# A graph layer on one core: SyncE fetches one of eight tiles of source rows of every eleventh chunk, row by row at addresses from registers

## The chip, the core and the metric

One core of a Trainium2 chip runs the whole kernel. The time is that of the device in microseconds, the median of the runs shown; a profile of one execution goes with it. TensorE is PE here (PEld its weight loads), VectorE DVE, ScalarE ACT, GpSimd POOL, and SyncE, which only issues DMAs, SP.

## What is computed

A graph with 6,250 nodes of 128 features and 200,000 edges, sorted by their destination. The layer is pre-normalized: `h = relu(layernorm(x))`, then two mesh convolutions and one edge-weighted attention, and the result is added to `x`. Cut to what matters:

```python
def mesh_conv(x, src, dst, ea, w1, b1, g, bt, w2, b2):
    m = concat([x[dst], x[src], ea]) @ w1 + b1        # per edge
    m = silu(group_norm(m, g, bt)) @ w2 + b2
    return segment_sum(m, dst) / clip(count(dst), 1)
...
q, k, v = h @ qw + qb, h @ kw + kb, h @ vw + vb
logits = (q[dst] * k[src]).sum(-1) * scale + ea @ ew + eb
w = softmax of logits over the edges of each dst
o = segment_sum(w * v[src], dst) @ ow + ob
```

The products with `w1` are done per node, so an edge needs the row of its source out of a table in DRAM: 128 numbers (512 bytes) in the convolutions, keys and values (1 KB) in the attention. The source is random, the destination sorted.

## The kernel before

**Tiles.** The edges stand in tiles of 128 (an edge a partition), 1,563 in all, and eight tiles make a chunk: 196 chunks, the last of three tiles. Three stages go over all chunks: `conv(1)`, `conv(2)` (L1003) and the attention (L1206 on). Each runs `pipeline` (L744), whose loop takes one step a chunk: it fetches the chunk two ahead, does the first product of the next chunk, the first half of this one, and the second half of older ones, and now and then a piece of a node batch (finished nodes, four windows of 128, every eighth step in the later part of a stage). At its end `in_order` (L732) fixes the order of DVE, SP, ACT and PE as written.

**Source rows.** `gather` (L648) issues one indirect DMA on POOL per tile (L650), which reads 128 indices from `src_i` in SBUF and fetches a row for each into tile `g`. POOL isn't in the list of `in_order`; it runs ahead as far as buffers allow: four of `g` in the convolutions, eleven in the attention. In the convolutions DVE adds `g` to the product (L1046); in the attention DVE multiplies its first half with the queries (L1258) and its second with the weights (L1314).

**Destination rows.** `loads` (L626) is SP's part of a step. It loads a register with the chunk's first node (`value`, L607) and fetches 112 rows from there into one of three tiles `pk` (L636). Every second step `load_group` (L614) loads for two chunks the relative destinations, broadcast to 112 partitions (`ohT`, L620, 896 KB), and the edge attributes (L623). ACT turns them into a one-hot matrix (`compared`, L645 and L646), and PE multiplies the two (L1039, in the attention L1243). PE also sums the edges of each node (L1071 and L1321). In the attention SP also loads, every eight steps, 16 rows of masks back to back (`load_runs`, L1272). SP also reads and stores the tables of the node batches (L882 to L948).

**Order on SP.** SP issues in program order. Where a DMA must wait for a buffer (L636 for a product of the chunk that used `pk` before, L620 for the group before last), all later ones wait behind it. The DMAs that SP issues take their completion semaphores in turn from eight, so that each also waits for the one eight before it.

Of the kernel before, what the change touches and what calls it, by code (L numbers as in the profile page):

```python
# [8 lines left out]
FP = mybir.dt.float32  # L9
BF = mybir.dt.bfloat16  # L10
I32 = mybir.dt.int32
# [4 lines left out]
SP = mybir.EngineType.SP  # L16
# [5 lines left out]
P = 128  # L22
D = 128
# [4 lines left out]
TPC = 8  # L28
# [4 lines left out]
LG = 2  # L33
WN = 112
SOON = 24
TAILS = [7, 7, 6, 5, 4, 3, 4]
BY_ACT = 60
KE = 5
KW = WN + KE
DB = D + H  # L40
PITCH = D + 4
VK = H * (HD + 1)
KV = 2 * D
# [6 lines left out]
def kernel(ctx: ExitStack, tc: tile.TileContext, x, src, dst, eat, w, out):  # L50
# [9 lines left out]
    nc = tc.nc  # L60
    N = x.shape[0]
    EI = src.shape[1]
    NCH = -(-EI // TPC)
# [5 lines left out]
    const = ctx.enter_context(tc.tile_pool(name="const", bufs=1))  # L69
# [7 lines left out]
    hpc = gpc.enter_context(tc.tile_pool(name="hpc", bufs=1))  # L77
# [43 lines left out]
    rows = {}  # L121

    def load_row(queue, name):
        v = w[name]
        rows[name] = const.tile([P, D], FP, name=f"r_{name}")
        queue.dma_start(
            out=rows[name], in_=bass.AP(tensor=v.tensor, offset=v.offset, ap=[[0, P], [1, D]]))

# [15 lines left out]
    b_d = {i: dram.tile([NW * P, D], FP, name=f"b_d{i}") for i in (1, 2)}  # L144
    kv_d = dram.tile([NW * P, KV], FP, name="kv_d")
    wc_d = {i: dram.tile([KE, D], FP, name=f"wc_d{i}") for i in (1, 2)}
    web_d = dram.tile([KE, DB], FP, name="web_d")
    dwl_d = dram.tile([P, EW], FP, name="dwl_d")
# [46 lines left out]
    with tc.tile_pool(name="node0", bufs=1) as np_, tc.tile_pool(name="prep", bufs=1) as pp, \  # L195
# [8 lines left out]
        step = 8  # L204
# [38 lines left out]
        for a in range(0, NW, 4):  # L243
            m = min(4, NW - a)
# [17 lines left out]
            o = pso.tile([P, 4, P], FP, name="o")  # L262
# [24 lines left out]
        for a, (m, tT) in keep.items():  # L287
            o = pso.tile([P, 4, P], FP, name="o")
# [50 lines left out]
        nc.vector.memset(t, 0.0)  # L339

    temb = hpc.tile([P, D], FP, name="temb")
    squares = {n: const.tile([P, D], FP, name=f"w_{n}") for n in ("c1_w2", "c2_w2", "ow")}
    qkv_t = const.tile([P, 3, D], FP, name="qkv_t")

    def spread(i):

        sizes, n = (TAILS[::-1], G) if i == 3 else ([GC] + [1] * 4, GC)
        rest, out = NCH, []
        while rest:
            out.insert(0, min(rest, sizes.pop(0) if sizes else n))  # L350
            rest -= out[0]
        return out

    def steps_of(i):


        ends, due, n = {}, {}, 0
        for m in spread(i):
            ends[n + m] = list(range(n, n + m))
            due.setdefault(n + m + (n < NCH - (sum(TAILS) if i == 3 else SOON)), []).extend(ends[n + m])  # L360
            n += m
        waiting, todo, left = [], [], NCH
        while left:
            n = len(todo)
            waiting += due.get(n, ())
            steps = min([m for m in due if m > n], default=n + 1) - n
            k = -(-len(waiting) // steps)
            todo.append(waiting[:k])
            waiting = waiting[k:]
            left -= k  # L370
        return ends, todo
# [239 lines left out]
    class Chunk:  # L611
        oh = None

    def load_group(c, pools):  # L614

        n = min(LG, NCH - c)
        m = min(n * TPC, EI - c * TPC)
        t = pools["ohT"].tile([P, LG, EPC], FP, name="ohT")
        f = t.rearrange("p c e -> p (c e)")
        nc.sync.dma_start(  # L620
            out=f[:WN, :m * P],
            in_=rel_d[c * TPC:c * TPC + m, :].rearrange("t p -> (t p)")[None, :].to_broadcast([WN, m * P]))
        nc.sync.dma_start(out=f[WN:KW, :m * P], in_=eat[:, c * EPC:c * EPC + m * P])  # L623
        pools[c // LG] = t
# [20 lines left out]
        nc.scalar.activation(k.ohT[:WN, :], k.ohT[:WN, :], AF.Square, bias=minus_p[:WN])  # L645
        nc.scalar.activation(k.ohT[:WN, :], k.ohT[:WN, :], AF.Relu, bias=1.0, scale=-4.0)  # L646

    def gather(k, g, table_d):  # L648
        for t in range(k.nt):
            nc.gpsimd.indirect_dma_start(  # L650
                out=g[:, t, :table_d.shape[1]], out_offset=None, in_=table_d,
                in_offset=bass.IndirectOffsetOnAxis(ap=k.src[:, t:t + 1], axis=0))
# [20 lines left out]
    def leftovers(body, pools):  # L673
# [9 lines left out]
        def one(c):  # L683
# [3 lines left out]
            with tc.For_i(0, n, 1) as r:  # L687
                k = Chunk()
                k.nt = TPC
                k.ea = lp.tile([KE, EPC], FP, name="l_ea")  # L690
                if isinstance(c, int):
# [52 lines left out]
    def pipeline(i, stage, aside=iter(())):  # L744

        start = len(nc.cur_bb.bb.instructions)
        ends, todo = steps_of(i)
        starts = {n: j for j, (n, _) in enumerate(plans[i])}
        ahead = stage.ahead
        ks, under_way, said = {}, [], {}
        for c in range(ahead):
            ks[c] = stage.fetch(c)
            compared(ks[c])
        stage.products(ks[0])
        for n, seconds in enumerate(todo):  # L760
            if n + ahead < NCH:
                ks[n + ahead] = stage.fetch(n + ahead)
            if n + 1 < NCH and stage.soon:
                stage.products(ks[n + 1])
            run = [ks[c] for c in ends.get(n, ())]
            stage.root(run)
            if n + ahead < NCH and stage.soon:
                compared(ks[n + ahead])
            first = (lambda k: lambda: stage.first(k))(ks[n]) if n < NCH else None
            if stage.second(run, [ks.pop(c) for c in seconds], first) and first:  # L770
                first()
            stage.finish()
            if n + ahead < NCH and not stage.soon:
                compared(ks[n + ahead])
            if n + 1 < NCH and not stage.soon:
                stage.products(ks[n + 1])
            if n < NCH:
                stage.early(ks, n, todo[n + 1])
            if n in starts:
                for _ in aside:  # L780
                    pass
                under_way.append(stage.batch(starts[n]))
            for g in list(under_way):
                if said.get(g) == "held" and n + 1 in ends:
                    continue
                said[g] = next(g, STOP)
                if said[g] is STOP:
                    under_way.remove(g)
            if n > 4:
                next(aside, None)  # L790
            if n < NCH:
                stage.reduce(ks[n])
        stage.flush()
        for g in (*under_way, aside):
            for _ in g:
                pass
        in_order(start)


    class Nodes:  # L800


        def __init__(self, pool, bank):
            self.pool, self.bank = pool, bank
# [198 lines left out]
    def conv(i):  # L1003
# [4 lines left out]
        with ExitStack() as es:  # L1008
            pool = lambda n, b, **kw: es.enter_context(tc.tile_pool(name=f"{n}{i}", bufs=b, **kw))
            pools = {"ohT": pool("ohT", 2), "oh": pool("oh", 2),  # L1010
                     "ps": pool("ps", 1, space=PSUM)}
# [12 lines left out]
                nc.vector.tensor_copy(t, s)  # L1024
            np_, nd = pool("np", 1), pool("nd", 1, space=PSUM)
            nodes = Nodes(np_of(np_, "A", "o"), lambda: nd.tile([P, BN, D], FP, name="nd", tag="nd"))
            side = es.enter_context(ExitStack())
            aside = iter(())
            if i == 1:
# [53 lines left out]
            class Stage:  # L1083
                ahead, soon = 2, True
                sums, late, roots, next = [], [], False, 0
                var, j, sd = None, 0, None

                def fetch(self, c):
                    k = loads(c, pools, a_d[i], self.ahead)
                    k.g = gp.tile([P, TPC, D], FP, name="g")  # L1090
                    gather(k, k.g, b_d[i])
                    k.h = hs[c % len(hs)]
                    return k

# [68 lines left out]
                    add_late(self.sums[0])  # L1163

            stage = Stage()
            nodes.var = lambda: stage.var[:, NV:]
            pipeline(i, stage, aside)
            side.close()
            pools["left"] = pool("left", 1)

            wcl = pools["left"].tile([KE, D], FP, name="wcl")
            nc.sync.dma_start(out=wcl, in_=wc_d[i])
# [28 lines left out]

    conv(1)
    conv(2)
    gpc.close()

# [5 lines left out]
    with ExitStack() as es:  # L1211
        pool = lambda n, b, **kw: es.enter_context(tc.tile_pool(name=f"{n}a", bufs=b, **kw))
        pools = {"oh": pool("oh", 2), "ps": pool("ps", 1, space=PSUM)}
# [156 lines left out]
        class Stage:  # L1370
            ahead, soon = 2, False
            sums, late, nb = [], [], None
            lg, j = None, 0

            def __init__(self, bp):
                self.bp = bp
                self.runs = list(steps_of(3)[0].values())
                self.nb = load_runs(self.runs.pop(0), bp)

            def fetch(self, c):  # L1380
                k = loads(c, pools, a_d[3], self.ahead)
                k.g = gp.tile([P, TPC, KV], FP, name="g")
                gather(k, k.g, kv_d)
                return k

            def products(self, k):
# [13 lines left out]
            def early(self, ks, n, then):  # L1400

                if then and then[0] >= NCH - BY_ACT:
                    onehot_by_act(ks[then[0]])
# [62 lines left out]
                merge_late(self.sums[0])  # L1466
                add_late(self.sums[0])

        with tc.tile_pool(name="bpa", bufs=1) as bp, tc.tile_pool(name="ohTa", bufs=2) as pools["ohT"]:
            pipeline(3, Stage(bp))  # L1470

        pools["left"] = pool("left", 1)
        webl = pools["left"].tile([KE, DB], FP, name="webl")
        nc.sync.dma_start(out=webl, in_=web_d)
# [79 lines left out]
```

## Time and profile before

| | |
|---|---|
| runs | 8,065.72, 8,086.02 and 8,091.16 us; median 8,086.02 |
| the profiled execution | 8,089.77 us, of which its span is 8,088.0 |
| mean granted TensorE clock | 0.681 |
| first convolution, second, attention (first to last gather) | 57 to 2,508 us, 2,590 to 5,004, 5,084 to 7,946 |
| DVE busy | 5,029 us in 7,337 instructions |
| POOL busy | 4,472 us in 4,703 instructions, 4,689 of them gathers |
| software queue (the gathers) | 175,056 packets, 410 MB |
| SP's hardware queue | 232,644 packets, 380 MB |

How to read the views: a group's line has its line in the code, engine, operation, out<-in and count; then busy us and mean ns of one; then the idle time of the engine just before these instructions and what ended most of it. "issue" is idle time that ended without anything visible to the profile, "remote" an ending that it can't place. In a list of waits: who waited, for whom, us in total, times, longest. In a timeline: start, duration, engine and line, and in brackets the idle time before it. SP counts as busy in no total; its issues stand in timelines as SPq. Times in timelines count from the start of the span.

### The profile page before, as it was taken

What the parts mean: (1) busy time and instruction counts of PE and PEld (TensorE: products, weight loads), DVE (VectorE), ACT (ScalarE), POOL (GpSimd) and SP (SyncE); (2) the same over time, 40 slices, a digit from 0 to 9 for tenths busy, and PEclk for the clock granted to TensorE, in tenths of its full rate; (3) what the DMA queues carried; (4) which work ended last, traced back from release to release, by engine and by line L of the source; (5) the groups of instructions that cost most, each with busy time, mean ns of one, the idle gap of its engine ahead of it and who ended that gap; (6) DMA issues with size and microseconds to landing.
All of it is one profiled execution on the core that took longest, in us unless ns stands there. A gap on an engine that the chain in (4) does not pass through costs nothing. (4 is left out here: it accounts for less than half of the span.)

```text
span 8088.0 us, 72425 instructions
## 1 busy us (share of the span) xinstructions
PE 3991.9 (49%) x20913; PEld 3669.4 (45%) x20914; DVE 5029.4 (62%) x7337; ACT 3488.4 (43%) x5607; POOL 4472.4 (55%) x4703
## 2 busy tenths in 40 slices
PE   4555554555544455555555554345444455455444
PEld 3445444444444444444544444244444444444434
DVE  5667776666665566666766666255655556565446
ACT  4555555555544455555555554122222222234444
POOL 5666666556653666666666553455554545555441
PEclk7676667777776666666777767666666666666666
DMA  5333333333322333333333332334444434444331
GB/s 135 102 95 93 88 106 85 91 87 89 90 79 60 92 88 92 87 89 91 101 96 96 95 92 67 109 111 116 123 115 116 116 112 115 120 121 121 110 105 54
DMA packets 413751, 798.16 MB, mean 99 GB/s; under 512 B 101571, under 2 KB 274742, under 8 KB 379285
## 3 DMA queue, kind: packets, MB, share of 16 engines
q0 software_dynamic: 175056, 410.03, 19.0%
q1 hardware_dynamic: 232644, 379.78, 16.5%
q10 hardware_dynamic: 5632, 3.50, 0.2%
q8 instruction: 173, 2.83, 0.2%
q14 instruction: 246, 2.02, 0.1%
HBM read 751.96 MB, written 40.96 MB: 98 GB/s over the span
## 5 line engine op out<-in xcount | busy, mean ns | idle before, releaser
L650 POOL DMA_INDIRECT g<-b_d,src_i x3126 | 2966.2, 949 | 1918.1 <-DVE h L1046 984.4
L650 POOL DMA_INDIRECT g<-kv_d,src_i x1563 | 1485.7, 951 | 1398.0 <-DVE cm L1357 828.3
L1071 PE MATMUL u<-h,oh 128*128 128x129 f32 (+1 forms) x6252 | 1337.3, 384 | 1723.0 <-ACT h L1066 897.0
L1071 PEld LDWEIGHTS u<-h,oh 128*128 128x128 f32 x6252 | 1204.7, 287 | 1841.0 <-ACT h L1066 939.6
L1039 PE MATMUL m<-pk,ohT 117*128 117x128 f32 x6252 | 1079.4, 327 | 665.0 <-issue 621.1
L1039 PEld LDWEIGHTS m<-pk,ohT 117*128 117x128 f32 x6252 | 1000.2, 241 | 723.2 <-issue 695.4
L1321 PE MATMUL us<-v,oh 128*128 128x145 f32 x3126 | 735.9, 396 | 930.1 <-issue 586.9
L1321 PEld LDWEIGHTS us<-v,oh 128*128 128x128 f32 x3126 | 645.7, 278 | 1007.7 <-issue 981.7
L1046 DVE TENSOR_TENSOR h<-m,g 128x1024 f32<-128x1024 f32 x392 | 475.1, 1212 | 951.0 <-remote 878.1
L1243 PE MATMUL qe<-pk,ohT 117*128 117x136 f32 x3126 | 586.4, 353 | 432.9 <-issue 238.6
L1243 PEld LDWEIGHTS qe<-pk,ohT 117*128 117x128 f32 x3126 | 545.9, 257 | 471.2 <-issue 275.3
L645 ACT ACTIVATE ohT<-ohT,minus_p 112x1024 f32<-112x1024 f32 x588 | 670.5, 1140 | 47.7 <-DMA ohT<-rel_d 30.3
L1066 ACT ACTIVATE h<-h 128x1024 f32<-128x1024 f32 x392 | 412.8, 1053 | 596.9 <-issue 308.8
L646 ACT ACTIVATE ohT<-ohT 112x1024 f32<-112x1024 f32 x588 | 619.7, 1054 | 18.6
L1076 ACT ACTIVATE u<-u,mask 128x129 f32<-128x129 f32 (+1 forms) x784 | 263.6, 336 | 807.9 <-remote 764.9
L1050 DVE TENSOR_REDUCE var<-sq 128x64 f32<-128x1024 f32 x392 | 475.2, 1212 | 170.5 <-ACT sq L1048 71.7
L656 DVE TENSOR_TENSOR oh<-cps,dm 128x1024 f32<-128x1024 f32 x392 | 474.6, 1211 | 56.1 <-remote 51.6
L1334 ACT ACTIVATE us<-d 128x16 f32<-128x16 f32 x196 | 36.7, 187 | 1067.5 <-DVE d L1331 782.0
L1064 DVE TENSOR_TENSOR h<-h,cps 128x1024 f32<-128x1024 f32 x392 | 477.2, 1217 | 13.4
L1065 DVE TENSOR_TENSOR h<-h,cps 128x1024 f32<-128x1024 f32 x392 | 477.1, 1217 | 13.4
L1048 ACT ACTIVATE sq<-h 128x1024 f32<-128x1024 f32 x392 | 411.3, 1049 | 162.4 <-DVE h L1046 130.9
L1061 DVE TENSOR_TENSOR h<-h,cps 128x1024 f32<-128x1024 f32 x392 | 474.4, 1210 | 0.0
(275 smaller groups left out, 4431.2 us busy)
## 6 DMA issues: line engine op xcount, KB each, us to landing
ohT<-rel_d SPq DMA_DIRECT2D x291, 896.0 KB
g<-b_d,src_i POOLq DMA_INDIRECT x3126
pk<-a_d SPq DMA_DIRECT2D x588, 56.0 KB
g<-kv_d,src_i POOLq DMA_INDIRECT x1563
ohT<-in_eat_dram SPq DMA_DIRECT2D x291, 40.0 KB
a_d<-n_o SPq DMA_DIRECT2D x28, 256.0 KB
kv_d<-n_o SPq DMA_DIRECT2D x28, 256.0 KB
n_h<-h_d SPq DMA_DIRECT2D x19, 256.0 KB
```

The costliest lines, as they stand in the source:

```text
L645: nc.scalar.activation(k.ohT[:WN, :], k.ohT[:WN, :], AF.Square, bias=minus_p[:WN])
L646: nc.scalar.activation(k.ohT[:WN, :], k.ohT[:WN, :], AF.Relu, bias=1.0, scale=-4.0)
L650: nc.gpsimd.indirect_dma_start(out=g[:, t, :table_d.shape[1]], out_offset=None, in_=table_d, in_offset=bass.IndirectOffsetOnAxis(ap=k.src[ ...
L656: return nc.vector.tensor_tensor(k.oh[:, :k.nt, :], iota[:, None, :].to_broadcast([P, k.nt, P]), k.dm[:, :, None].to_broadcast([P, k.nt, P ...
L1039: nc.tensor.matmul(k.m[:, t, :], lhsT=lhs[:, t * P:(t + 1) * P], rhs=rhs, start=(j == 0), stop=(j == len(terms) - 1))
L1046: nc.vector.tensor_tensor(k.mt, k.m[:, :n], k.g[:, :n], ALU.add)
L1050: return lambda: nc.vector.tensor_reduce(var[:, at:at + n * H], sq[:, :n].rearrange("p t (g c) -> p (t g) c", c=HD), AX.X, ALU.add)
L1064: nc.vector.tensor_tensor(k.mt, k.mt, over_edges(gam, k.nt), ALU.mult)
L1065: nc.vector.tensor_tensor(k.mt, k.mt, over_edges(bet, k.nt), ALU.add)
L1071: nc.tensor.matmul(k.u[:, 0, :wide], lhsT=k.oh[:, t, :], rhs=k.h[:, t, :wide], start=(t == 0), stop=(t == k.nt - 1))
L1243: nc.tensor.matmul(k.qe[:, t // TB, at:at + DB], lhsT=lhs[:, t * P:(t + 1) * P], rhs=rhs, start=(j == 0), stop=(j == len(terms) - 1))
L1321: nc.tensor.matmul(k.u[:, :wide], lhsT=k.oh[:, t, :], rhs=k.v[:, t, :wide], start=(t == 0), stop=(t == k.nt - 1))
```

## The change

Chunks 16, 27, 38 ... 192 (17 of the 196 in each stage) lose the gather of their eighth tile. In its place SP fetches the 128 rows one by one: in each of eleven steps it loads up to twelve indices into registers and issues as many DMAs of one row each into a tile `row_g`; in the step before the chunk is used ACT copies that tile into the eighth part of `g`. The rows of a chunk are fetched in steps 13 to 3 before its own, and the next chunk's follow at once, so that 187 of the 196 steps of a stage have them. Within a step they come after `fetch` (the `pk` and `ohT` loads) and before the first product. The indices lie in a [1, 128] tile that SP loads from the input one chunk ahead. To make room, weight tiles that nothing reads once the second convolution is done move to a pool that is given back then. In the program as built SP's list has 6,528 row DMAs, 51 loads of indices and 561 register loads more, and 6,528 fused register operations that work out the addresses; POOL's has 17 gathers less in each stage.

```diff
+ROWS = 12
...
+    def by_rows():
+
+        span, first = -(-P // ROWS), LG + 3
+        return list(range(first + span, NCH - 1, span)), span
+
+    class Rows:
...
+        def __init__(self, pool, table_d, width):
+            self.pool, self.table_d, self.width = pool, table_d, width
+            self.chunks, self.span = by_rows()
+            self.starts = {c - 2 - self.span: c for c in self.chunks}
+            self.now, self.got = None, {}
+            self.at = {}
+            if self.chunks:
+                self.list_of(self.chunks[0])
+
+        def list_of(self, c):
+            t = self.pool.tile([1, P], I32, name="row_at")
+            col = c * TPC + TPC - 1
+            nc.sync.dma_start(out=t, in_=src[:, col:col + 1].rearrange("p o -> o p"))
+            self.at[c] = t
+
+        def step(self, n):
+            if n in self.starts:
+                c = self.starts[n]
+                self.now = [c, 0, self.pool.tile([P, self.width], FP, name="row_g")]
+                self.got[c] = self.now[2]
+                j = self.chunks.index(c) + 1
+                if j < len(self.chunks):
+                    self.list_of(self.chunks[j])
+            if self.now:
+                c, e, t = self.now
+                m = min(ROWS, P - e)
+                _, at = nc.values_load_multi_w_load_instructions(
+                    self.at[c][0:1, e:e + m], engines=[SP], min_val=0, max_val=N - 1,
+                    skip_runtime_bounds_check_because="a source node")
+                for j, a in enumerate(at):
+                    nc.sync.dma_start(out=t[e + j:e + j + 1, :], in_=self.table_d[bass.ds(a, 1), :self.width])
+                self.now[1] = e + m
+                if e + m == P:
+                    self.now = None
+
+        def put(self, k):
+            if k.c in self.got:
+                nc.scalar.copy(k.g[:, TPC - 1, :self.width], self.got.pop(k.c))
...
-    def gather(k, g, table_d):
-        for t in range(k.nt):
+    def gather(k, g, table_d, lone=()):
+        for t in range(k.nt - bool(lone and k.c in lone)):
...
                 ks[n + ahead] = stage.fetch(n + ahead)
+            stage.rows.step(n)
             if n + 1 < NCH and stage.soon:
...
                 stage.early(ks, n, todo[n + 1])
+            if n + 1 < NCH:
+                stage.rows.put(ks[n + 1])
```

In the changed file the row DMAs stand at L653, their register load at L649, the copy at L660, the gathers at L698, the `pk` load at L684 and the `ohT` load at L668.

More of the change, by code (lines that the diff above doesn't have):

```diff
@@ L124, in load_row @@
         v = w[name]
-        rows[name] = const.tile([P, D], FP, name=f"r_{name}")
+        rows[name] = (const if name in ("ob", "an_g", "an_b") else hpc).tile([P, D], FP, name=f"r_{name}")
         queue.dma_start(
@@ L341 @@
     temb = hpc.tile([P, D], FP, name="temb")
-    squares = {n: const.tile([P, D], FP, name=f"w_{n}") for n in ("c1_w2", "c2_w2", "ow")}
-    qkv_t = const.tile([P, 3, D], FP, name="qkv_t")
+    squares = {n: (const if n == "ow" else hpc).tile([P, D], FP, name=f"w_{n}") for n in ("c1_w2", "c2_w2", "ow")}
+    qkv_t = hpc.tile([P, 3, D], FP, name="qkv_t")
     def spread(i):
@@ L1026, in conv @@
             nodes = Nodes(np_of(np_, "A", "o"), lambda: nd.tile([P, BN, D], FP, name="nd", tag="nd"))
+            rw = pool("rw", 2)
             side = es.enter_context(ExitStack())
@@ L1090, in fetch @@
                     k.g = gp.tile([P, TPC, D], FP, name="g")
-                    gather(k, k.g, b_d[i])
+                    gather(k, k.g, b_d[i], self.rows.chunks)
                     k.h = hs[c % len(hs)]
@@ L1165, in conv @@
             stage = Stage()
+            stage.rows = Rows(rw, b_d[i], D)
             nodes.var = lambda: stage.var[:, NV:]
@@ L1376, in __init__ @@
                 self.bp = bp
+                self.rows = Rows(rw, kv_d, KV)
                 self.runs = list(steps_of(3)[0].values())
@@ L1382, in fetch @@
                 k.g = gp.tile([P, TPC, KV], FP, name="g")
-                gather(k, k.g, kv_d)
+                gather(k, k.g, kv_d, self.rows.chunks)
                 return k
@@ L1467, in flush @@
                 add_late(self.sums[0])
-        with tc.tile_pool(name="bpa", bufs=1) as bp, tc.tile_pool(name="ohTa", bufs=2) as pools["ohT"]:
+        with tc.tile_pool(name="bpa", bufs=1) as bp, tc.tile_pool(name="rwa", bufs=2) as rw, \
+                tc.tile_pool(name="ohTa", bufs=2) as pools["ohT"]:
             pipeline(3, Stage(bp))
```

## The prediction

> **What bounds the kernel now.** First the page: the busy shares, and the two groups of gathers that the change thins out.
>
> ```profile
> span 8088.0 us, 72425 instructions
> ...
> PE 3991.9 (49%) x20913; PEld 3669.4 (45%) x20914; DVE 5029.4 (62%) x7337; ACT 3488.4 (43%) x5607; POOL 4472.4 (55%) x4703
> ...
> L650 POOL DMA_INDIRECT g<-b_d,src_i x3126 | 2966.2, 949 | 1918.1 <-DVE h L1046 984.4
> L650 POOL DMA_INDIRECT g<-kv_d,src_i x1563 | 1485.7, 951 | 1398.0 <-DVE cm L1357 828.3
> ```
>
> No engine is full. POOL starts a gather every 1.25 us (0.95 and a gap of 0.30), ten us for a chunk of eight, and then sits idle 984 us for DVE's add and 828 us for the attention's last reader: it waits for a free buffer. The view of the gathers' own line says who waits for them:
>
> ```profile
> who waited for it (us, times):
>   DVE h L1046: 47.0, 8
>   POOL g L650: 43.6, 143
>   DVE g L1258: 17.0, 2
> ```
>
> Only 64 us in ten waits, in three stages. Pairing each chunk's last gather with its first reader in the trace, the gather ends a median of 38 and 37 us before the add in the two convolutions (never under 25, but 8.6 at the second one's chunk 0) and 25 us before the attention's product (under 6 at its first two chunks alone). POOL is about three conv chunks ahead; it isn't the bound.
>
> What is then? The timeline of PE in the second convolution shows a product of 16 matmuls that should take 2 us (as it does when unhindered) drawn out over 14:
>
> ```profile
> 3558.77 0.27 PE L1039 MATMUL m<-pk,ohT 117*128 117x128 f32 x1 [1.91 <-issue]
> 3560.87 0.27 PE L1039 MATMUL m<-pk,ohT 117*128 117x128 f32 x1 [1.83 <-issue]
> ...
> 3566.47 0.37 PE L1039 MATMUL m<-pk,ohT 117*128 117x128 f32 x1 [1.73 <-issue]
> ...
> 3572.77 2.78 PE L1039 MATMUL m<-pk,ohT 117*128 117x128 f32 x9 [0.33 <-issue]
> ```
>
> Weight loads and matmuls start at multiples of 0.70 us, and nothing visible holds them ("issue"). I call this pacing. The clock is no cause: mean grant 0.68, and 0.27 against 0.37 us a matmul is all that half a clock makes. Counting runs of at least five such ticks in PE's and SP's records gives 200 episodes, 1,990 us of the span; DVE and ACT run untouched meanwhile and then wait. SP is paced as well:
>
> ```profile
> 5700.03 7.80 SPq L1272 DMA_DIRECT2D nbs<-nbs_d  x6
> 5709.92 8.40 SPq L1272 DMA_DIRECT2D nbe<-nbe_d  x8
> ```
>
> Fourteen DMA issues in over 16 us, beside a paced PE. The same kind of burst late in the attention costs a third of a us an issue:
>
> ```profile
> 7576.43 2.32 SPq L1272 DMA_DIRECT2D nbs<-nbs_d  x7
> 7578.85 2.29 SPq L1272 DMA_DIRECT2D nbe<-nbe_d  x7
> ```
>
> Seventeen of those bursts in a row (5,354 to 7,124 us) took 18 to 21 us for 16 issues, in ticks of 0.70 or 1.40 us: PE and SP seem to take turns. Between episodes a conv step takes 8.5 us (adds at 3573.70 and 3582.22), near DVE's busy time; the average is 12.3. So a step is DVE's work plus pacing, and POOL fits under it. Last, SP's waits:
>
> ```profile
> SPq L620 <- remote: 2759.0, 155, 48.4
> SPq L636 <- remote: 1139.3, 88, 35.9
> ```
>
> With smaller ones SP waits some 5,500 us: about 4.3 us of a 13.7 us step are its own.
>
> **The change part by part.** *Removed:* 17 chunks (16, 27 ... 192) in each stage lose one gather: 51 x 1.25 = 64 us of POOL. At those chunks its lead is 11 us or more (25 in the convolutions), and its next wait is for the same buffer; I take 0, with 64 as the end of a gain.
>
> *Added on SP:* 51 x 128 = 6,528 row DMAs, 51 list loads and 561 register loads (11 steps a chunk, so 187 of a stage's 196 steps). A DMA with a register address leaves FUSED_REGOPS (37 ns), MOVE (29) and the DMA (322) in the rows of L636, 0.51 us to the next instruction with the gaps; a plain one in the unpaced burst above is 0.33. So 12 rows take 4.0 to 6.2 us; I take 6. One register load at L607 has a median of 0.46 us; here one fills twelve registers: 0.46 to 5.5, and I take 0.5, as it is one instruction on 48 adjacent bytes. Every SP DMA waits for the one eight before it, so rows behind an ohT load wait for its landing: the profile has 12.6 us in 5 such waits at L1272, 2.5 each, once in two steps. A step costs SP 6 + 0.5 + 1.2, nearly 8 us unpaced, beside 9.4 of waiting: it just fits. Behind the rows queue the next pk load (L636; issue to use: 5% under 14 us, median 24 in the convolutions) and ohT load (L620; issue to compare: quarter under 11.5 us, of which 5.4 is transfer), and the nodes' stores. Eight us of delay is hidden for pk and eats the quarter of ohT loads with least slack; without that cover each late load costs its lateness once in two steps.
>
> *Added elsewhere:* 51 ACT copies, between 0.39 (128x128 at L1367) and some 0.63 us (128x512, L826), under 32 us on an engine busy 43%; each waits for rows issued two steps before and gathers that lead by more; behind it queue the node batch's copies and the next step's SiLU. I take 0. The moved weight tiles change no instruction.
>
> *Pacing, the term that decides.* SP leaves 4,913 records now and PE 43,156 (weight loads, matmuls, its sequencer). The change adds 6,579 DMAs, 6,528 register operations, as many MOVEs and 561 loads, less 36 waits: 20,160, or 42% on the two engines that are paced. No row shows what pacing does with more SP work. Low end 0: episodes go by time, and SP only takes turns (where SP shared an episode of 20 ticks in the attention, PE issued 11 instructions in place of 15, and they were equally long). High end: every burst is paced as the seventeen were; 37 instructions at 0.70 to 1.40 are 26 to 52 us a step, twice the kernel. Between ends that far apart the nearest row is the present pacing per instruction of PE and SP, 1,990 / 48,069 = 41 ns; conv steps from 2,650 to 3,600 and attention steps have nearly the same, 58 and 59, while 1,000 to 2,500 has 32, so it is no constant. I take it as proportional: 0.42 x 1,990 = 836 us. Exposed are 0.82 of it: five steps of 11.9 us hold 17 us above five of 8.5, and 20.7 us of episodes.
>
> *Sum:* 8,089.8 (span 8,088.0 and 1.8 around it) - 0 + 0 + 0.82 x 836 = 8,775; the median shown is 4 lower, so **8,770 us**.
>
> [...] The trace shows no instruction fetch at the start of most episodes, and no row names the cause of the ticks.
>
> **The rivals.**
>
> *SP's work fits.* Pacing goes by time, rows fill SP's waits, only some ohT loads come late: a quarter of 280 loads by about 2 us is 140 us. 8,066 to 8,300. For it: 5,500 us of waiting, equally long shared episodes. Against: SP would be used to 90%.
>
> *All instructions share one limit.* The trace has 8.7 to 9.6 records a us over all engines in every steady stretch, though convolution and attention mix engines differently (PE 5.6 and 5.0 a us, DVE 1.2 and 2.1). At 72,425 / 8,088 = 8.95 a us, 20,160 and 340 on ACT cost 2,290 us: 10,380. Against: the steady rate varies by some 10%, and it needs POOL and DVE to count alike though they are never paced. [...]
>
> *Faster: pacing follows the gathers.* Episodes fill 35% of 2,650 to 3,600 us, where POOL's count is 638 in 950 us, and 20% of 1,000 to 2,500 (927 in 1,500): 9% more gathers, 15 points. A drop of 1.1% would take 1.8 points, 150 us: 7,940. With POOL's 64 us alone, 8,026. It decides if gathers, not PE and SP, raise the ticks; against it: SP, not POOL, is paced with PE.
>
> The change does what it says: in the built program each stage issues 1,546 gathers for 1,563, and the row DMAs stand in SP's list.
>
> **How the numbers follow.** Forecast (8,300 to 9,300, centre 8,770): 0.45. All share a limit, or rows add more pacing than in proportion (above 9,300): 0.22; 0.08 of it above 10,400. SP's work fits: 0.26, of which 0.10 within 24 us of the median (0.3%, about what a measurement of this kernel tells from no change) and 0.16 above. Faster: 0.07. So faster 0.07, same 0.10, slower 0.83. The range 8,080 to 10,400 leaves out the faster case, a third of the unchanged one and the 0.08 at the top; the forecast's own is 8,300 to 9,300.
>
> **What would show it.** Right: PE's idle "issue" at the matmul lines (823 + 621 + 587 + 239 = 2,270 now) grows by some 40%; POOL's idle grows by 64 us and more; L653's DMAs in SP's timeline come in ticks of 0.70 and 1.40 us as well as 0.5. If SP's work fits, "issue" stays and ACT's wait for ohT (30 us) grows. If all share a limit, records a us stay at 9 with a span over 10,000. If the register load takes 5 us, SP itself is full: pk loads are issued under 8 us before use, and PE waits for them. Wrong in kind: fewer paced ticks with fewer gathers.

## The result and the profile after

The changed kernel takes **8,639.85 us** (median of 8,629.35 to 8,656.88) beside 8,084.95 for the kernel before (four runs now, one more than in the table above): a ratio of 1.069, 95% interval 1.0668 to 1.0711, so it is slower by 555 us. The profiled execution took 8,656.88 us, of which 8,655.1 are its span.

The page of the changed kernel: first the busy line, then four groups.

```profile
span 8655.1 us, 92851 instructions
...
PE 3900.0 (45%) x20913; PEld 3684.5 (43%) x20914; DVE 5032.3 (58%) x7337; ACT 3495.4 (40%) x5658; POOL 4429.5 (51%) x4652
...
L698 POOL DMA_INDIRECT g<-b_d,src_i x3092 | 2939.5, 951 | 2355.4 <-DVE h L1098 1407.9
...
L698 POOL DMA_INDIRECT g<-kv_d,src_i x1546 | 1469.5, 950 | 1563.3 <-DVE cm L1410 939.5
...
L1091 PE MATMUL m<-pk,ohT 117*128 117x128 f32 x6252 | 1124.0, 350 | 1378.0 <-DMA pk<-a_d 604.0
...
L693 ACT ACTIVATE ohT<-ohT,minus_p 112x1024 f32<-112x1024 f32 x588 | 672.4, 1144 | 1577.3 <-DMA ohT<-rel_d 1384.9
```

The engines are about as busy as before (PE 2% less) and idle more. POOL waits still longer for a free buffer (1,408 and 940 us, from 984 and 828), so its saved 64 us bought nothing. The news is in the last two lines. The same two groups in the kernel before:

```profile
L1039 PE MATMUL m<-pk,ohT 117*128 117x128 f32 x6252 | 1079.4, 327 | 665.0 <-issue 621.1
...
L645 ACT ACTIVATE ohT<-ohT,minus_p 112x1024 f32<-112x1024 f32 x588 | 670.5, 1140 | 47.7 <-DMA ohT<-rel_d 30.3
```

Before, PE's first product waited for "issue", 621 us; now "issue" is 487 us, and 604 us more go to the destination rows' load. ACT waited 30 us for `ohT`; now 1,385. Both loads are SP's. Now SP's own waits, the four largest:

```profile
SPq L668 <- remote: 214.6, 10, 44.4
SPq L653 <- DMA ohT<-rel_d: 73.7, 74, 3.5
SPq L653 <- DMA row_g<-b_d: 59.8, 113, 1.4
SPq L684 <- remote: 55.0, 8, 32.2
```

Before, the first and the last were 2,759 and 1,139 us: SP stood ahead and waited for buffers. Now it hardly ever does: all its waits together were 5,805 us and are 810. Pairing each `pk` load with its product in the trace, SP issues it a median of 2.3, 1.9 and 6.2 us before its use in the three stages, where it was 24, 24 and 34. **SP's list has become the bound.** Its timeline in the first convolution shows why:

```profile
1505.39 0.33 SPq L684 DMA_DIRECT2D pk<-a_d  x1
1506.70 5.09 SPq L653 DMA_DIRECT2D row_g<-b_d  x12
...
1514.70 0.71 SPq L671 DMA_DIRECT2D ohT<-in_eat_dram  x1
1516.85 17.88 SPq L653 DMA_DIRECT2D row_g<-b_d  x12
1535.98 0.18 SPq L684 DMA_DIRECT2D pk<-a_d  x1
1537.15 20.14 SPq L653 DMA_DIRECT2D row_g<-b_d  x12
1558.12 0.32 SPq L684 DMA_DIRECT2D pk<-a_d  x1
```

Twelve rows take 5.09 us, and 17.88 and 20.14 when they meet ticks of 0.70 and 1.40 us. The `pk` load at 1558.12 stood behind the second of them. PE's timeline of the same stretch shows first the two engines taking turns, with matmuls 2.8 us apart (a weight load and a matmul at 1.40 us each), and then PE waiting 15.8 us for that load:

```profile
1518.60 1.39 PE L1091 MATMUL m<-pk,ohT 117*128 117x128 f32 x11
1520.45 0.35 PE L1091 MATMUL m<-pk,ohT 117*128 117x128 f32 x1 [0.45 <-issue]
1523.26 0.37 PE L1091 MATMUL m<-pk,ohT 117*128 117x128 f32 x1 [2.46 <-issue]
1526.08 0.37 PE L1091 MATMUL m<-pk,ohT 117*128 117x128 f32 x1 [2.44 <-issue]
...
1559.97 3.75 PE L1091 MATMUL m<-pk,ohT 117*128 117x128 f32 x16 [15.80 <-DMA pk<-a_d]
```

Counted as in the prediction, there are 327 episodes of 2,145 us (200 of 1,990 before). On SP alone, instructions that start 0.70 or 1.40 us after the one before fill 4,245 us, where they filled 713; 3,504 of these are at the row lines. A convolution step goes from 12.6 and 12.4 us to 13.6 and 13.5, an attention step from 15.0 to 15.8 (mean spacing of the adds and of the logits' sums), which from the first chunk of each stage to its last is 564 us, nearly all of the 567 by which the span grew.

### The profile page after: what moved, and what is told of

It reads as the page before. It is cut to its first block, busy times and chain, and to the rows that moved or that the text cites. A ratio compares the mean times of both kernels' runs of the same rounds, so it can differ in the third digit from the quotient of the medians.

```text
span 8655.1 us, 92851 instructions
## 1 busy us (share of the span) xinstructions
PE 3900.0 (45%) x20913; PEld 3684.5 (43%) x20914; DVE 5032.3 (58%) x7337; ACT 3495.4 (40%) x5658; POOL 4429.5 (51%) x4652
## 5 line engine op out<-in xcount | busy, mean ns | idle before, releaser
L698 POOL DMA_INDIRECT g<-b_d,src_i x3092 | 2939.5, 951 | 2355.4 <-DVE h L1098 1407.9
L698 POOL DMA_INDIRECT g<-kv_d,src_i x1546 | 1469.5, 950 | 1563.3 <-DVE cm L1410 939.5
L1123 PE MATMUL u<-h,oh 128*128 128x129 f32 (+1 forms) x6252 | 1234.9, 377 | 1475.8 <-ACT h L1118 898.1
L1123 PEld LDWEIGHTS u<-h,oh 128*128 128x128 f32 x6252 | 1153.9, 284 | 1550.3 <-ACT h L1118 940.4
L1091 PE MATMUL m<-pk,ohT 117*128 117x128 f32 x6252 | 1124.0, 350 | 1378.0 <-DMA pk<-a_d 604.0
L1091 PEld LDWEIGHTS m<-pk,ohT 117*128 117x128 f32 x6252 | 1054.0, 260 | 1436.2 <-issue 937.1
L1374 PE MATMUL us<-v,oh 128*128 128x145 f32 x3126 | 716.8, 409 | 655.5 <-DVE nm L1407 406.9
L1374 PEld LDWEIGHTS us<-v,oh 128*128 128x128 f32 x3126 | 664.4, 294 | 695.4 <-issue 675.4
L1311 DVE TENSOR_TENSOR g<-qe,g 128x768 f32<-128x768 f32 (+1 forms) x391 | 252.1, 686 | 903.6 <-remote 824.5
L1313 ACT COPY ebs<-qe 128x48 f32<-128x48 f32 (+1 forms) x391 | 53.4, 188 | 1084.0 <-DVE g L1311 1010.0
```

Source lines behind the costliest of these rows:

```text
L698: nc.gpsimd.indirect_dma_start(out=g[:, t, :table_d.shape[1]], out_offset=None, in_=table_d, in_offset=bass.IndirectOffsetOnAxis(ap=k.src[ ...
L1091: nc.tensor.matmul(k.m[:, t, :], lhsT=lhs[:, t * P:(t + 1) * P], rhs=rhs, start=(j == 0), stop=(j == len(terms) - 1))
L1123: nc.tensor.matmul(k.u[:, 0, :wide], lhsT=k.oh[:, t, :], rhs=k.h[:, t, :wide], start=(t == 0), stop=(t == k.nt - 1))
L1374: nc.tensor.matmul(k.u[:, :wide], lhsT=k.oh[:, t, :], rhs=k.v[:, t, :wide], start=(t == 0), stop=(t == k.nt - 1))
```

## The experiments

Two theories at the start. **S**: SP's list sets the step, by what the rows cost there. **I**: the forecast, ticks in proportion to PE's and SP's instructions. A third, **G**, came from the trace: 198 of the 200 episodes before, and 325 of the 327 after, begin inside an unbroken row of gathers. The experiments ran on four chips, and there the kernel before took 6,234 to 6,243 us instead of 8,085, which changed the question. Each ratio below is to the kernel before on the same chip.

**Half the gathers.**

```
-        for t in range(k.nt):
+        half = k.nt // 2 if getattr(k, 'c', 0) else 0
+        if half:
+            nc.gpsimd.memset(g[:, :half, :table_d.shape[1]], 0.0)
+        for t in range(half, k.nt):
             nc.gpsimd.indirect_dma_start(
```

> The kernel before, with half of each chunk's gathers left out (one memset on POOL zeroes those four tiles, so their edges' source rows are missing from the result); nothing changes on PE and SP. Theory G (pacing comes from gathers: in the kernel before, 198 of 200 episodes begin inside an unbroken row of gathers, a median of 17 us after its start, and end 3 us after it; in the changed kernel 325 of 327): a burst is now 4 or 8 gathers, 5 to 10 us, so episodes fall from 1,990 us to under 500 and the time by 0.82 of that, to 6,800 to 7,300 us. Theory I (pacing goes with the number of PE's and SP's instructions, as the prediction has it) and theory T (it goes by time): 8,050 to 8,090 us, with about 2,000 us of episodes.

5,587 us beside 6,237, ratio 0.896 (0.8942 to 0.8978). All expected times missed, for they supposed 8,086 and its ticks. No episode is found in this trace, and none was there to be removed, so it says nothing on G. It does show the next limit: with POOL thinned out DVE is busy for 90% of the span.

```profile
span 5589.0 us, 69683 instructions
...
PE 3318.5 (59%) x20913; PEld 3180.3 (57%) x20914; DVE 5007.8 (90%) x7337; ACT 3465.0 (62%) x5607; POOL 2689.5 (48%) x2957
```

**The gathers left out, and no rows for them** (in the changed kernel, beside the removed copy):

```
+        if lone and k.c in lone:
+            nc.gpsimd.memset(g[:, TPC - 1, :table_d.shape[1]], 0.0)
...
-                _, at = nc.values_load_multi_w_load_instructions(...)
-                for j, a in enumerate(at):
-                    nc.sync.dma_start(out=t[e + j:e + j + 1, :], in_=...)
```

> The changed kernel without the row DMAs, their register loads and the copies (a memset on POOL zeroes the 51 tiles, whose source rows are missing from the result); 51 list loads stay. This is what 51 gathers less are worth by themselves. Theory S (SP's own list sets the step now: pk loads are issued a median of 2 us before their use, where it was 24): without the rows SP waits again and the time is that of before less at most 64 us, 8,020 to 8,090. Theory G: 1% fewer gathers, 20 us of pacing, the same. A cause that lies elsewhere in the change (moved weight tiles, pools) would leave it above 8,150.

6,183.5 us, ratio 0.9916 (0.9900 to 0.9933): 53 us less, where 51 gathers of 1.25 us are 64 and the 51 memsets in their place take 13 us of POOL. The expected 8,020 to 8,090 again supposed ticks. On this chip gathers count nearly one for one; the moved weight tiles cost nothing that shows.

**Rows at constant addresses.**

```
-                _, at = nc.values_load_multi_w_load_instructions(...)
-                for j, a in enumerate(at):
-                    nc.sync.dma_start(out=t[e + j:e + j + 1, :], in_=...)
+                for j in range(m):
+                    a = (c * 128 + e + j) * 37 % N
+                    nc.sync.dma_start(out=t[e + j:e + j + 1, :], in_=self.table_d[a:a + 1, :self.width])
```

> The changed kernel with constant addresses: the same 6,528 row DMAs in the same places, but no register load, no fused register operation and no MOVE (so other rows than the right ones come in). Theory S: a step of SP holds 13 instructions less than 37 of the rows; unpaced 12 x 0.33 = 4 us, paced 8 to 17 us, and SP's lateness goes mostly: 8,100 to 8,300, with pk loads issued 10 us and more before use. Theory I: 6,630 added instructions, 14% of 48,069: 8,086 + 0.14 x 1,990 x 0.82 = 8,310, with PE's idle 'issue' up 14%. If the DMAs themselves cost (semaphores, queue), not the instructions: 8,600.

6,189 us, ratio 0.9925 (0.9909 to 0.9942). All three forecasts were for a chip with ticks. Without them 6,528 DMAs of 0.30 us (median from one to the next) fit into SP's waits and leave 47 of the 53 us that the gathers are worth.

**Rows on ACT's queue.**

```
-                    self.at[c][0:1, e:e + m], engines=[SP], min_val=0, max_val=N - 1,
+                    self.at[c][0:1, e:e + m], engines=[mybir.EngineType.Activation], min_val=0, max_val=N - 1,
...
-                    nc.sync.dma_start(
+                    nc.scalar.dma_start(
```

> The changed kernel with the row DMAs, register loads and register operations on ACT's instruction stream and ACT's DMA queue instead of SP's. ACT is busy 5.3 us of a 12.3 us step in the profile of before and shows no ticks of 0.70 us. Theory S: SP is as before, and ACT gets about 12 x 0.41 + 0.8 = 5.8 us a step more, which fits into its idle 7 us only in part, since its instructions are in order: 8,150 to 8,500. Theory I counts PE and SP alone: 8,090. If ACT's register instructions are paced as SP's are (36 at 0.70 us in an episode): above 8,700.

9,077 us, ratio 1.455 (1.4529 to 1.4578), on a chip without ticks: over every forecast but "above 8,700", whose ground (ticks on ACT) isn't there either. What I had left out is the wait for landings. One burst in ACT's timeline:

```profile
2002.20 11.71 ACTq L653 DMA_DIRECT2D row_g<-b_d  x12
2013.93 1.28 ACT L1109 ACT_TABLE_LOAD   x1 [11.58 <-DMA row_g<-b_d]
```

Here twelve rows hold ACT for 11.7 us, at the median 8.0. The MOVEs at that line take 2,120 us from one start to the next in place of the 189 that they are busy; with them the rows and their register loads fill 4,753 us of ACT, beside the 3,484 that it is busy. And PE waits 3,493 us for ACT's SiLU, where the changed kernel without ticks (below) has 1,467. SP can stand in such waits because it runs ahead (531 us of them for `ohT` in the changed kernel without ticks, and `pk` still issued 17 to 19 us before use in the convolutions); ACT is in the step's chain.

**The changed kernel and the kernel before, unedited, and sixteen rows a step** (`ROWS = 16`; 23 tiles a stage).

> The changed kernel itself, unedited, beside the kernel before on one chip, because in the last four runs the kernel before took 6,237 us and no run showed ticks of 0.70 us on SP or PE. Theory P (the ticks come from the chip's condition, not from the kernel; where they are absent POOL's 8 x 1.25 = 10 us set a convolution step, and SP's 12 x 0.41 + 0.8 + 1.2 = 7 us fit beside them): 6,180 to 6,240 where the kernel before takes 6,237, and again about 8,640 where it takes 8,086. Theory S' (the rows cost by themselves, ticks or not): over 6,400 beside 6,237.

> The kernel before, unedited, for its trace. Theory P: if its time is near 6,237, POOL has hardly any idle time with a releaser (DVE's add and the attention's reader had 984 and 828 us), DVE waits for gathers, and no episodes of ticks are found; if near 8,086, some 200 episodes as before. Theory G (bursts of gathers cause the ticks) has to explain why bursts that are longer still cause none.

> The changed kernel with sixteen rows a step in place of twelve: every eighth chunk instead of every eleventh, 23 tiles a stage instead of 17, 69 gathers less in all. Theory P: where POOL sets the step and SP's 16 x 0.41 + 0.8 + 1.2 = 8.6 us still fit into 10, the gain grows with the gathers, 69 x 1.25 = 86 us: 6,150 to 6,200; where ticks are present SP's list is longer by a third of the rows: 8,750 to 8,900. Theory S': slower than the changed kernel in both.

The changed kernel took 6,201 us beside 6,243: **0.9934 (0.9917 to 0.9951)**, a gain of 0.7%. The kernel before, 6,234.66 us in its profile:

```profile
span 6232.9 us, 72425 instructions
...
L650 POOL DMA_INDIRECT g<-b_d,src_i x3126 | 2971.5, 951 | 968.5 <-issue 872.5
...
L650 POOL DMA_INDIRECT g<-kv_d,src_i x1563 | 1487.7, 952 | 524.4 <-issue 439.6
...
L1046 DVE TENSOR_TENSOR h<-m,g 128x1024 f32<-128x1024 f32 x392 | 476.3, 1215 | 502.0 <-DMA g<-b_d,src_i 476.2
```

The roles are exchanged. POOL's idle time before gathers is the 0.30 us between two (4,306 times in all, 1,312 us), and DVE's add waits for gathers, 476 us. A convolution step takes 10.0 us, eight gathers of 1.25. No episode is found, here or in the changed kernel, so theory P (the ticks don't come from the kernel, and without them POOL sets the step) holds in all three of its signs. G alone doesn't explain the ticks: here the rows of gathers run on for over a thousand (88 at most in the two traces with ticks, gaps under 0.4 us), and none appear. The same timeline of SP in the changed kernel, without ticks:

```profile
1513.01 0.32 SPq L684 DMA_DIRECT2D pk<-a_d  x1
...
1515.01 4.80 SPq L653 DMA_DIRECT2D row_g<-b_d  x12
1520.64 0.32 SPq L684 DMA_DIRECT2D pk<-a_d  x1
...
1524.26 6.11 SPq L653 DMA_DIRECT2D row_g<-b_d  x12
```

The 6.11 is a burst behind an `ohT` load, whose landing a row waits for (282 such waits in this trace, 531 us). All row lines take 3,354 us and the register loads 514, 6.9 us for each of 561 steps; the profile with ticks has 5,901 and 482, 11.4 us.

Sixteen rows gave 6,682 us, ratio 1.0697 (1.0679 to 1.0715), against the expected 6,150 to 6,200. The waits are those of the 8,640 us, with no ticks at all:

```profile
ACT ohT L693 <- DMA ohT<-rel_d: 1114.7, 213, 12.2
```

That wait is 36 us with twelve rows. SP is full here by its own work: rows and register loads take 4,248 + 649 us, 8.9 a step where I had 16 x 0.41 + 0.8 = 7.4, and with the 1.2 that the prediction gives the other loads that is over ten. `pk` is issued a median of 2.8 to 4.6 us before use.

**Six rows a step** (`ROWS = 6`; 8 tiles a stage) **and a memset ahead of each gather** (kernel before).

```
+    idle = const.tile([P, 1], FP, name="idle")
...
+            nc.gpsimd.memset(idle, 0.0)
             nc.gpsimd.indirect_dma_start(
```

> The changed kernel with six rows a step: a tile takes 22 steps, so 8 chunks a stage lose a gather instead of 17, and SP's rows take 6 x 0.41 + 0.6 = 3.1 us a step instead of 5.7. Theory P, where the kernel before takes about 6,240 us: POOL sets the step, 24 gathers less are 24 x 1.25 = 30 us, and nothing is late: 6,205 to 6,225. Where it takes about 8,090: SP's list is the bound only if it overflows, and half the rows don't (18 instructions in an episode at 0.70 to 1.40 are 13 to 25 us in one step of three, 3 us in the others, against 9.4 us of waits): 8,090 to 8,300, not half of the 555 us that twelve rows cost. A cost in proportion to the rows would give 8,340.

> The kernel before with one small memset on POOL (128 x 1) ahead of each gather, so that gathers come at least 0.15 us further apart; nothing is left out. Theory P, where the kernel before takes about 6,240 us: POOL's period sets the time, and 4,689 memsets of 0.10 us with their gaps cost nearly all of their own time: 6,800 to 7,700, and the longer period shows in the gathers' spacing. If POOL were not the bound there: under 6,400. Where the kernel before takes about 8,090: POOL's lead of 25 us hides it all, 8,070 to 8,150, unless the bursts of gathers cause the ticks (theory G): then fewer episodes and under 7,900.

Six rows: 6,209 us, ratio 0.9957 (0.9941 to 0.9974); 26 us less for 30 us of gathers, as expected. The memsets: 6,929 us, ratio 1.1109 (1.1091 to 1.1128), as expected in size. POOL's order isn't fixed, and they went in bunches (mostly of 49 to 63 in the first convolution, all ahead of 570 us) instead of one ahead of each gather, so the spacing of gathers stayed at 1.25 us and G stayed untested. POOL's total is what counts:

```profile
L652 POOL MEMSET idle<- 128x1 f32 x4689 | 467.1, 100 | 341.4 <-DVEq L668 39.1 <-SPq L668 36.6
```

467 busy and 341 idle, 808 us on POOL, of which 693 show in the time: POOL is the bound there.

**Sixteen rows ahead of the step's other loads, sixteen at constant addresses, and the changed kernel again.**

```
+            stage.rows.step(n)
             if n + ahead < NCH:
                 ks[n + ahead] = stage.fetch(n + ahead)
-            stage.rows.step(n)
```

> Sixteen rows a step as before, but a step issues its rows ahead of its pk and ohT loads, so that the DMA eight before a row is no ohT load just issued (SP's rows waited 463 us in 271 waits for ohT's landing with sixteen rows, 531 us in 282 with twelve). Theory P: where the kernel before takes about 6,240 us, SP's list with sixteen rows overflowed by those waits, 6,682 - 463 = 6,220, and near there POOL takes over again with 86 us less of gathers: 6,150 to 6,230. If the overflow is SP's issue alone: 6,550 to 6,690. Where the kernel before takes about 8,090: 8,750 to 8,900 with ticks on SP.

> Sixteen rows a step, in the old place, with constant addresses: no register load, register operation or MOVE (other rows than the right ones come in). Where the kernel before takes about 6,240 us: if SP's instructions make sixteen rows overflow, 16 x 0.13 + 1.24 = 3.3 us a step are gone, nothing is late, and 69 gathers less show in full: 6,150 to 6,185. If the DMAs or their landings do: over 6,500. Where it takes about 8,090: SP's part of an episode is a third, 8,100 to 8,400.

> The changed kernel itself once more, on whichever chip this call gets. Theory P: 0.99 to 1.00 of the kernel before where that takes about 6,240 us without ticks, 1.06 to 1.08 where it takes about 8,090 with them, and nothing in between.

The first took 6,670 us, ratio 1.0693 (1.0675 to 1.0711), as if nothing had been moved: the rows' wait for `ohT` fell only from 463 to 344 us, and 84 us went to the masks' loads. So most of the waits were still there, and by itself this says little on my theory that they made the overflow. The second settles it: 6,177 us, ratio 0.9909 (0.9892 to 0.9925), 57 us less for 86 us of gathers, with as many DMAs and even 1,018 us of waits for `ohT`; rows take 6.9 us a step in place of 8.9. What overflows SP is the work on registers around each DMA. The third: 6,199 us, 0.9941 (0.9925 to 0.9958), the same small gain on another chip.

No kernel with the right rows was clearly faster than the changed one without ticks. None of the edited kernels ran with ticks; six rows there stay untried.

## Why the prediction was right, and where it wasn't

8,640 us lies in the range, inside the forecast's own 8,300 to 9,300, and 130 us from its centre. The sign and the size came out. The step that gave the size didn't.

- **POOL isn't the bound; the saved gathers are worth 0.** Right where it was forecast: POOL's idle grew. On the chips of the experiments it is wrong: 35 to 53 us of the 64 come through (0.9916 without rows, 0.9934 and 0.9941 with them). The rival "POOL's 64 us alone" is what happens there.
- **SP's added work without ticks, 6 + 0.5 us a step.** About right: 5.1 for a burst and 0.8 for the register load (0.76 the load itself), and 1.0 more for landings. "It just fits" held without ticks, and `pk` kept a lead of 17 to 19 us in the convolutions. Two readings were a little off: the list of SP's waits adds up to 5,805 us and not 5,500, and 10% of the convolutions' `pk` loads, not 5%, had under 14 us.
- **"Pacing, the term that decides": 42% more instructions, 836 us more of it, 0.82 exposed.** This step failed. Episodes grew by 8%, not 42%. The sign that was to show it, PE's idle "issue" at the four matmul lines up by 40%, went the other way: 576 + 487 + 160 + 73 = 1,296 us, from 2,270. What the ticks did was to stretch SP's own list, from 6.9 us a step for rows and register loads to 11.4, in which other loads queue. SP ran out of its 9.4 us of waiting, and PE and ACT then waited for loads, 604 + 166 and 1,385 us. The prediction had the pieces (bursts of 16 drawn out to 20 us; "26 to 52 us a step" as the high end; pk loads under 8 us before use as the sign of a full SP) but put SP's filling down to a slow register load alone and charged the ticks to PE by a ratio. That 8,770 came near is luck of the ratio.
- **SP's work fits (0.26).** False with ticks; true on the chips of the experiments.
- **All instructions share one limit (10,380).** Refuted: with 92,851 records the steady stretches have 10.3 to 11.8 a us, where 8.7 to 9.6 was to be the ceiling.
- **Pacing follows the gathers.** 1% fewer gathers brought no fewer episodes. That almost all begin in rows of gathers stays true of both traces; longer rows without ticks show that it isn't enough.
- **"No row names the cause of the ticks."** That stands, and no trace shows that they are instruction fetch. The added instructions by themselves cost little without ticks: 20,426 more records, the row "q14 instruction" up from 246 to 406 packets in both conditions, and a ratio of 0.9934 beside 0.9916 without the rows. With ticks the same two programs are 555 us apart.

**Open:** what causes the ticks. They stand in the two traces of the result and none of those of the experiments, the same two programs among them; whether they belong to a chip or to its state at the time is not settled. A lower granted clock alone doesn't bring them: rows on ACT ran at 0.685 without any. Nor is memory slower with them: the gathers' packets took 19.0% of 8,088 us with ticks and 25.6% of 6,233 without, 1,537 and 1,596 us. The account of the 8,640 us rests on its own two traces, without an edited kernel among ticks, and on sixteen rows, which fill SP in another way and bring the same waits.

## What to carry to other kernels

A queue that runs ahead has its slack written in its own waits: when it waits for buffers there is room, and when those waits are gone whatever stands behind new work on it is late (here SP's waits went from 5,805 to 810 us, and the lead of `pk` in the first convolution from 24 to 2.3 us). Price added DMA issues with the instructions around them (0.41 us a row here, 0.30 at a constant address), in us of that queue's step, once by the undisturbed issue and once by the slowest that the trace shows, and hold both against that queue's waits before any ratio (here 7 and 26 to 52 us, and 11.4 measured, against 9.4 of waits). And when an idle time ends in "issue" on a grid with no cause in view, ask what the kernel does without it: here that exchanges the bound (POOL for SP and PE) and with it the sign of the change.

## What the runs showed of the hardware

- The same kernel took 8,085 us with ticks of 0.70 us on PE and SP, and 6,234 to 6,243 without; the mean granted clock was 0.681 and 0.771. In the ticks PE and SP start an instruction every 0.70 or 1.40 us, in turn where both have work (PE's matmuls then 2.8 us apart, SP's twelve rows in 17.88 and 20.14 us), while the gathers on POOL keep their 0.95 us.
- Without ticks a DMA of SP with its address in a register costs 0.41 us to the next (register operation, MOVE, DMA; median), one with a constant address 0.30.
- Loading SP's registers isn't in proportion to their number: without ticks medians of 0.99 us for six, 0.76 for twelve and 1.18 for sixteen.
- SP's DMAs take completion semaphores in turn from eight: in the changed kernel's trace with ticks 8,361 of 8,414 have the semaphore of the DMA eight before. Without ticks its rows waited 282 times for a load of 896 KB, of which there are 294, 1.9 us each.
